# Who issues the first loads, and in which order VectorE, TensorE and GpSimd start, in an attention and expert kernel

## The chip, the cores and the metric

The kernel runs on one core of a Trainium2 chip. A core has five engines with an instruction queue each: TensorE (PE, matmuls and transposes), VectorE (DVE), ScalarE (ACT), GpSimd (POOL) and SyncE (SP), which in this kernel does nothing but issue DMAs. An engine works through its queue strictly in order: an instruction that waits for a semaphore holds up all that stands behind it. The DMAs themselves run on 16 DMA engines. The metric is the time of one execution in microseconds (us); lower is better.

## The reference

`x` is (8, 512, 256), float32. The reference does two residual blocks:

```
x = x + layernorm(attention(layernorm(x)))      # 16 heads of 16
x = x + layernorm(experts(layernorm(x)))        # 8 experts, top 1
```

The attention is not the usual one: the weights of each row are summed over the keys (`einsum('blmh,blhd->blhd')`), so that a head needs only the sum of its softmax row times its own `v`. The scores, their row maximum, the exponential and its sum must still be computed for 8 batches, 16 heads and 512 x 512 scores. The expert block is one shared matrix `wi` (256 to 1024) with a rank-4 correction of the chosen expert, a relu, and `wo` (1024 to 256).

## The kernel before

All matmuls are float32. Where precision asks for it a tensor is split into a high part (type fp32r) and a low part, and three products are summed: high by high, high by low, low by high (`three`, around L486). That is why names come in pairs: `wqkh`/`wqkl`, `xnh`/`xnl`, `wih`/`wil`.

**The stages of one batch b.** `prepare` normalises `x[b]`: the statistics `st_x_b` (4 pieces, L399) and `mv_x_b` (L404) on VectorE, the reciprocal root `nr_x_b` on GpSimd, the scaled `ln_x_b` (on VectorE for batch 0, on GpSimd for the others), a transpose on TensorE (`pst_xn`, L469), and the split into `xnh` (ScalarE, L521) and `xnl` (VectorE, L528). `project` multiplies by `wqk`, four products of 512 columns, each 6 matmuls: `psqk_b_g_t`, with g for the heads 0 to 7 or 8 to 15 and t = 0 for q, 1 for k. Each is split into `hl_b_g_t`; for batch 0 the high half is ScalarE's (L362) and the low half VectorE's (L375). `lay_out_q` and `lay_out_k` are DMAs from SBUF to SBUF: they put the rows of two heads, a pair p of 8, where the score matmul wants them. `rows_b_p` (L572, two DMAs) are the keys. The queries are `q_0_p` (L593, two DMAs) for the first 256 tokens of batch 0, and elsewhere a ring of six tiles q0 to q5 (L606, four DMAs each). `scores` then runs for each pair p and each 128 tokens: the score matmuls (`sc`, L651 for `q_0_p`, L642 for the ring), the negated row maximum `nmax` on VectorE (L661), and the exponential with its row sum on ScalarE (L670). A name such as `nmax_0_3_1_1` is batch 0, pair 3, token block 1, second head of the pair. `values`, `attend` and `feed` are the rest: `psv` and `v`, the division and the output projection `psy`, the gate (`wga`), and the expert matmuls `psh` and `psz`. A weight is split once at the start: `wvh`, `wvl`, `wouth`, `woutl`, `wih`, `wil`, `woh`, `wol` on GpSimd (L298, L306), `wqkl` and the LoRA factors `lbh`, `lbs` on VectorE (L306, L1166, L1171).

**What sets the order.** A planner (`Plan.order`) lists all operations by a model of costs and due times. `settle` then rewrites the start of that list by hand. Its helper `behind(last, ops)` takes `ops` out of the list and puts them directly after `last`. Each engine runs its own operations in the order of the list; the position of an operation therefore only counts against others of the same engine, and `behind` an operation of another engine means: at that place of the list. In the changed version `k0` and `q0`, `q1`, `k1` are the low halves of `hl_0_0_1`, `hl_0_0_0`, `hl_0_1_0` and `hl_0_1_1`. In the list of before, SyncE issues x of batch 0 in two halves, `wqk` in two, `bqk`, then `wv_0`, `wout_0`, `lb`, four `wi`, `xt_1` to `xt_3`, six small ones, then `q_0_0`, `rows_0_0`, `q_0_1`, `rows_0_1`, the four `wo`, `q_0_2`, `rows_0_2`, `rows_0_3` and so on.

**Two things that the list doesn't show.** Each DMA reports its landing on one of eight counters, which the framework hands out in turn, in the order of the list; a DMA whose counter is still owed by the DMA eight places earlier waits at its queue for that landing. And the PSUM tiles named `w` (for `pst`, `psqk`, `psv` and others) are three, used in turn: a fourth product waits until the first has been read. The scores have five.

The constants that the change touches or uses: `XB = 4` tiles of x, `X1B = 3` tiles for `q_0_p`, `QB = 6`.

Of the kernel before, what the change touches and what calls it, by code (L numbers as in the profile page):

```python
# [26 lines left out]
PE, ACT, DVE, POOL, DMA = "PE", "ACT", "DVE", "POOL", "DMA"  # L27
# [155 lines left out]
def kernel(  # L183
# [18 lines left out]
    nc = tc.nc  # L202
# [45 lines left out]
    def const_tile(shape, dtype, name, parts=1):  # L248
        return plan.tile(const, shape, dtype, name, 1, name)
# [6 lines left out]
    behind = [0.0]  # L256

    def landing(size):

        behind[0] = max(0.0, behind[0] + size / DMA_RATE - DMA_COST)  # L260
        return DMA_DELAY + size / DMA_RATE + behind[0]

    def load_x(b):
        t = xts[b] = plan.tile(io, [P, NC, D], F32, "xt", XB, f"xt_{b}")
        m = X0 if b == 0 else NC
        for c in range(0, NC, m):
            plan.op(
                DMA, DMA_COST,
                lambda c=c: nc.sync.dma_start(
                    out=t()[:, c : c + m],  # L270
                    in_=x[b].rearrange("(p c) d -> p c d", c=NC)[:, c : c + m],
                ),
                writes=[t], lag=landing(m * P * D * 4),
            )

    def load(name, src, shape=None, rows=P, place=None):

        shape = shape or list(src.shape)
        if place is None:
            t = const_tile(shape, F32, name)  # L280
        else:
            t = plan.tile(place[0], shape, F32, *place[1:], name)
        plan.op(
            DMA, DMA_COST, lambda: nc.sync.dma_start(out=t()[:rows], in_=src), writes=[t],
            lag=landing(rows * np.prod(src.shape[1:]) * 4),
        )
        return t

    def on_all_partitions(name, src):
        return load(name, src.partition_broadcast(P), [P, src.shape[0]])  # L290
# [23 lines left out]
    def fetch(name, src, *places):  # L314

        fs = flat(src).rearrange("p (c d) -> p c d", d=D)
        return [
            load(f"{name}_{i}", fs[:, 2 * i : 2 * i + 2], [P, 2, D], place=places[i % len(places)])
            for i in range(fs.shape[1] // 2)
        ]  # L320
# [23 lines left out]
    for i in range(2):  # L344
        t = const_tile([P, 2 * P], F32R, f"axs{i}")
# [146 lines left out]
    def units(b):  # L492

        return (0, 1), (2, 3)
# [590 lines left out]
    def fetch_first():  # L1085
        parts = [
            load(f"wqk_{dc}", wqk[:, dc], [P, 2, NG, P], place=(work, "full", FB))
            for dc in range(ND)
        ]
        return load("bqk", bqk), parts  # L1090

    during(-9000, "first", load_x, 0)
    wqk_in = during(-8990, "first", fetch_first)
    during(5000, "warm", warm_up)
# [36 lines left out]
    for g in range(NG):  # L1131
        during(-7000 if g == 0 else 0, f"project0{g}", project, 0, g)
        for p in range(NP * g, NP * (g + 1)):
            during(-6000 + 2 * p, "k0", lay_out_k, 0, p)
    during(0, "x1", load_x, 1)
    wv_h, wv_l = during(0, "wv", weight, "wv", wv.shape, wv_in, (POOL, POOL))

# [46 lines left out]
    for b in range(B):  # L1184
        t = 2 * STEPS * b
        if b + 2 < B:
            behind[0] = 0.0
            during(t, "load", load_x, b + 2)

        apart = units(b) if b in APART else [(0, 1, 2, 3)]  # L1190
        for i, cs in enumerate(apart):
            for p in range(NPR):
                at = t + STEPS * i + p * len(cs)
                during(at if b or i else at - 6000, "q" if b or i else "q0", lay_out_q, b, p, cs)
                scores(b, cs, p, at)
        if b + 1 < B:
            during(t, "prepare", prepare, b + 1)
            for g in range(NG):
                during(t, f"project{g}", project, b + 1, g)
                for p in range(NP * g, NP * (g + 1)):  # L1200
                    n = 2 if b + 1 in APART else 4
                    during(t + n * p, "k", lay_out_k, b + 1, p)
        for u in range(len(units(b))):
            tu = t + STEPS * (u if b in APART else 1)
            left = 2 * B - 1 - (2 * b + u)
            k = f"_{left}" if left < 3 else f"_first{u}" if b == 0 else f"{u}"
            during(tu, "v" + (k if b == 0 else ""), values, b, u)
            during(tu, "attend" + k, attend, b, u)
            during(tu, "feed" + k, feed, b, u)

    def settle(done):


        def of(eng, *marks):
            return [o for mark in marks for o in done if o.eng == eng and o.mark == mark]

        def behind(last, ops):
            for o in ops:
                done.remove(o)
            i = done.index(last) + 1  # L1220
            done[i:i] = ops


        behind(of(DVE, "ln_x_0_2")[-1], of(DVE, "bqk"))
        lbh = of(DVE, "lbh_0", "lbh_512")
        behind(of(DVE, "xnl_0")[-1], lbh)
        st2, turns = of(DVE, "st_x_2"), of(DVE, "hl_0_0_0", "hl_0_0_1", "hl_0_1_0")
        st1, maxes = of(DVE, "st_x_1"), of(DVE, "nmax_0_0_1_1", "nmax_0_2_0_1")
        behind(turns[0], st1[:2])
        behind(turns[1], st1[2:] + of(DVE, "mv_x_1"))  # L1230
        behind(turns[2], st2[:2])
        behind(maxes[0], st2[2:] + of(DVE, "mv_x_2"))
        behind(of(DVE, "nmax_0_2_0_1")[0], of(DVE, "st_x_3", "mv_x_3"))
        lbs = of(DVE, "lbs")
        behind(of(DVE, "nmax_0_1_1_1")[0], lbs[:1])
        behind(of(DVE, "nmax_0_3_0_1")[0], lbs[1:])
        behind(of(DVE, "nmax_0_4_1_1")[0], of(DVE, "wga"))


        nr = [[o for o in done if o.eng == POOL and o.mark == f"nr_x_{i}"] for i in range(4)]  # L1240
        wih, wil = of(POOL, "wih"), of(POOL, "wil")
        woh, wol = of(POOL, "woh"), of(POOL, "wol")
        behind(of(DVE, "mv_x_1")[-1], nr[1] + [wih[2], wil[2], wih[3], wil[3]])
        behind(of(DVE, "mv_x_2")[-1], nr[2])
        behind(of(POOL, "ln_x_2_2")[-1], nr[3])
        behind(
            [o for o in of(POOL, "ln_x_3_0")][-1], [woh[0], wol[0], woh[1], wol[1]]
        )
        behind(of(POOL, "hl_1_0_0")[-1], [woh[2], wol[2], woh[3], wol[3]])
        calm = Op()  # L1250
        calm.eng, calm.mark = POOL, None
        calm.fn = lambda: nc.gpsimd.tensor_scalar(
            calm_sb(), state[0]["xn"]()[:, 1, :1], 1.0, 0.0, ALU.mult, ALU.add
        )
        last = of(DVE, "ln_x_0_2")[-1]
        early = [o for o in done[done.index(nr[0][-1]) + 1 : done.index(last)] if o.eng == POOL]
        behind(last, early)
        done.insert(done.index(last) + 1, calm)


        rows = []
        for p in range(NP):
            if p < X1B:
                rows += of(DMA, f"q_0_{p}")
            rows += of(DMA, f"rows_0_{p}")
            if p == 1:
                rows += of(DMA, "wo_0", "wo_1", "wo_2", "wo_3")
        behind(turns[1], rows)


        extra = of(PE, "psu")[FIRST:]
        return [o for o in done if o not in extra]

    done = settle(plan.order())

    name = f"{B - 1}_{units(B - 1)[-1][0]}"
# [3 lines left out]
    i = [k for k, o in enumerate(done) if o.mark == f"mv_z_{name}_1"][-1] + 1  # L1280
# [66 lines left out]
DMA_COST = 440.0  # L1347
# [20 lines left out]
XB = 4  # L1368
HLB = 6
RB = 8  # L1370
QB = 6
# [69 lines left out]
```

## Time and profile before

| | |
|---|---|
| median of three runs | 516.54 us (516.49 to 519.35) |
| the profiled execution | 513.44 us |
| its span, from the first to the last instruction | 511.6 us |
| mean granted TensorE clock | 0.963 |
| TensorE, VectorE, ScalarE, GpSimd busy | 483.8, 467.3, 436.4, 390.1 us |
| the first score matmul starts | 21.11 us |
| the first exponential starts | 22.37 us |
| DMA issues on SyncE, each | 0.33 to 0.60 us |

The profile's page gives busy time by engine, the span in 40 equal slices of 12.8 us (a digit is the busy share in tenths; `PEclk` the clock that TensorE was granted), and the chain of work that ended last. Other views of the same trace list the instructions in order of time, the waits by who waited for whom, and the busy time in stretches that one chooses. A busy TensorE is not TensorE at full speed: a matmul that takes twice as long at half the clock counts as twice as busy.

### The profile page before, as it was taken

How to read it: one execution, taken by the hardware profiler on the slowest of the kernel's cores; microseconds unless marked ns; L12 is line 12 of the kernel's file. 1: busy time of each engine (PE TensorE's matmuls, PEld its weight loads, DVE VectorE, ACT ScalarE, POOL GpSimd, SP SyncE). 2: the span in 40 equal slices, each digit the busy share in tenths (PEclk: the TensorE clock that was granted, in tenths of full speed). 3: DMA queues.
4: the chain of work that ended last, by engine and by line, in shares of the span. 5: the costliest groups of instructions: out<-in, count | busy, mean ns of one | idle time of the engine just before them, and what ended most of it. 6: DMA issues, size and time to landing. Idle time of an engine off the chain costs nothing.

```text
span 511.6 us, 11203 instructions
## 1 busy us (share of the span) xinstructions
PE 483.8 (95%) x3134; PEld 423.7 (83%) x3134; DVE 467.3 (91%) x1056; ACT 436.4 (85%) x1205; POOL 390.1 (76%) x615
## 2 busy tenths in 40 slices
PE   7769989999999999999999999999999999998995
PEld 6534837879888988989989988989899988998995
DVE  6788999999999999999999999999999999998633
ACT  3569999998999999998999899999999989995210
POOL 7867455565889987997979998696878767888652
PEclk9955879999999999999999999999999999999999
DMA  8772263334423443244423442244224432200001
GB/s 273 217 196 68 52 154 71 89 69 112 111 51 106 113 111 68 69 121 104 105 50 120 101 102 75 51 113 110 66 70 94 114 87 67 48 26 2 21 22 42
DMA packets 41182, 46.56 MB, mean 91 GB/s; under 512 B 11326, under 2 KB 28222, under 8 KB 41120
## 3 DMA queue, kind: packets, MB, share of 16 engines
q1 hardware_dynamic: 41120, 45.84, 35.2%
q8 instruction: 26, 0.43, 0.3%
q14 instruction: 36, 0.29, 0.2%
HBM read 8.05 MB, written 4.19 MB: 24 GB/s over the span
## 4 chain that ended last, share of the span: by engine, by line
PE 62%; DVE 24%; ACT 4%; DMA 3%; issue 2%; SPq 2%; POOL 1%; POOLq 0%; ACTq 0%; DVEq 0%
PE sc L642 16%; PE psz L486 14%; DVE nmax L661 13%; PE psh L486 12%; PE psqk L486 7%; PE psy L486 3%; ACT sc L670 3%; PE psv L486 3%; PE psh L960 2%; DVE st_x L399 2%; PE sc L651 1%; DMA q<-hl 1%; DMA rows<-hl 1%; DVE hTh L300 1%; PE pst_x L469 1%
## 5 line engine op out<-in xcount | busy, mean ns | idle before, releaser
L670 ACT ACTIVATE sc<-sc,nmax 128x512 f32<-128x512 f32 x512 | 342.6, 689 | 17.1 <-DVE nmax L661 10.6
L661 DVE TENSOR_REDUCE nmax<-sc 128x1 f32<-128x512 f32 x512 | 325.4, 678 | 9.2 <-PE sc L651 4.2
L642 PE MATMUL sc<-rows,q 128*128 128x512 f32 x480 | 182.6, 423 | 5.6 <-ACT sc L670 3.1
L670 ACT ACTIVATION_READ_ACCUMULATOR sc<-sc,nmax 128x1 f32 x512 | 120.6, 236 | 0.0
L642 PEld LDWEIGHTS sc<-rows,q 128*128 128x128 f32 x480 | 88.7, 192 | 25.7 <-ACT sc L670 18.7
L486 PE MATMUL psz<-woh,hTh 128*128 128x256 f32 x256 | 73.0, 285 | 0.8 <-DVE xnl L528 0.5
L486 PE MATMUL psh<-x2h,wih 128*128 128x256 f32 x256 | 73.0, 285 | 0.0
L486 PE MATMUL psz<-woh,hTl 128*128 128x256 f32 x256 | 72.2, 282 | 0.0
L486 PE MATMUL psz<-wol,hTh 128*128 128x256 f32 x256 | 72.1, 282 | 0.0
L486 PE MATMUL psh<-x2h,wil 128*128 128x256 f32 x256 | 72.0, 281 | 0.0
L486 PE MATMUL psh<-x2l,wih 128*128 128x256 f32 x256 | 72.0, 281 | 0.0
L306 POOL TENSOR_TENSOR hTl<-full_h,hTh 128x512 fp32r<-128x512 f32 x44 | 56.9, 1294 | 2.3 <-DVE hTh L300 1.1
L486 PEld LDWEIGHTS psz<-wol,hTh 128*128 128x128 f32 x256 | 48.2, 188 | 3.6
L486 PEld LDWEIGHTS psh<-x2l,wih 128*128 128x128 f32 x256 | 48.2, 188 | 3.2
L486 PEld LDWEIGHTS psz<-woh,hTh 128*128 128x128 f32 x256 | 48.2, 188 | 2.1 <-POOL hTl L306 0.7
L486 PEld LDWEIGHTS psh<-x2h,wih 128*128 128x128 f32 x256 | 48.3, 189 | 1.1 <-DVE y L777 0.2
L486 PEld LDWEIGHTS psz<-woh,hTl 128*128 128x128 f32 x256 | 48.2, 188 | 0.2 <-POOL hTl L306 0.2
L486 PEld LDWEIGHTS psh<-x2h,wil 128*128 128x128 f32 x256 | 48.2, 188 | 0.0
L306 POOL TENSOR_TENSOR hl<-full_qk,hl 128x512 fp32r<-128x512 f32 x28 | 36.3, 1295 | 1.2
L384 ACT ACTIVATE full_h<-psh 128x512 f32<-128x512 f32 x44 | 26.4, 605 | 8.6 <-PE psh L960 8.1
L298 POOL TENSOR_SCALAR hl<-full_qk 128x512 fp32r<-128x512 f32 x28 | 17.3, 619 | 18.2 <-ACT full_qk L384 17.5
L486 PE MATMUL psqk<-xnh,wqkh 128*128 128x512 f32 x64 | 27.6, 431 | 0.7 <-ACT xnh L521 0.7
(132 smaller groups left out, 1021.4 us busy)
## 6 DMA issues: line engine op xcount, KB each, us to landing
rows<-hl SPq DMA_DIRECT2D x128, 128.0 KB, 2.6
q<-hl SPq DMA_DIRECT2D x480, 32.0 KB, 2.0
out<-ln_z SPq DMA_DIRECT2D x15, 256.0 KB, 2.2
xt<-in_x SPq DMA_DIRECT2D x7, 512.0 KB, 3.8
wi<-in_wi SPq DMA_DIRECT2D x4, 256.0 KB, 6.4
q<-hl SPq DMA_DIRECT2D x16, 64.0 KB, 2.2
wo<-in_wo SPq DMA_DIRECT2D x4, 256.0 KB, 4.5
xt<-in_x SPq DMA_DIRECT2D x2, 256.0 KB, 2.7
```

What stands on the lines that cost most here:

```text
L298: nc.gpsimd.tensor_scalar(pick_hi(), pick(), 1.0, 0.0, ALU.mult, ALU.add)
L300: nc.vector.tensor_copy(pick_hi(), pick())
L306: e.tensor_tensor(pick_lo(), pick(), f32(pick_hi()), ALU.subtract)
L384: lambda: nc.scalar.activation(full(), flat(ps()), func, **kw()),
L399: DVE, 335, lambda c=c: nc.vector.bn_stats(st()[:, c, :], sel()[:, c, :]),
L469: nc.tensor.transpose(ps()[:, dc, c * P : (c + 1) * P], src()[:, c, dc * P : (dc + 1) * P], ident(),)
L486: nc.tensor.matmul(ps, w, xx, start=start and i == 0, stop=stop and i == len(terms) - 1)
L642: nc.tensor.matmul(sc(), q()[:, e, cols], k(), start=True, stop=True)
L651: nc.tensor.matmul(sc(), q()[rows, 0, cols], k()[rows], start=True, stop=True)
L661: lambda sc=sc, nmax=nmax: nc.vector.tensor_reduce(nmax(), sc(), AX.X, ALU.max, negate=True),
L670: lambda sc=sc, nmax=nmax, esum=esum, i=i, h=h: nc.scalar.activation(sc(), sc(), AF.Exp, bias=nmax(), accum_out=esum()[:, i, h : h + 1]),
L960: nc.tensor.matmul(ps()[:, i, :], lbs()[:KL, fs], axs()[:KL, : n * P], start=False, stop=i == 1,)
```

## The change

Ten loads (`wv_0`, `wout_0`, `lb`, the four `wi`, `xt_1`, `xt_2`, `xt_3`) are issued by ScalarE's queue; the other loads stay on SyncE's. All 21 of them come directly behind `bqk`, and the four `wo` no longer stand between `rows_0_1` and `q_0_2`. The layout DMAs of pairs 0 to 3 stand behind `hl_0_0_1` rather than behind the first `hl` that is ready. VectorE gets another order of its first work, TensorE takes `psv` ahead of the last two `psqk`, ScalarE likewise `v` ahead of the last two `hl`, GpSimd takes `ln_x_1` ahead of the last `wi` splits. Later layout DMAs are exchanged: `q_0_6` and `q_0_7` come earlier, and the first 24 DMAs of the ring go tile by tile. Nothing is computed differently.

```diff
@@ load_x
-                lambda c=c: nc.sync.dma_start(
+                lambda c=c: (nc.scalar if 0 < b < XB else nc.sync).dma_start(
@@ load
+        queue = nc.scalar if name.split("_")[0] in ("wv", "wout", "lb", "wi") else nc.sync
...
-            DMA, DMA_COST, lambda: nc.sync.dma_start(out=t()[:rows], in_=src), writes=[t],
+            DMA, DMA_COST, lambda: queue.dma_start(out=t()[:rows], in_=src), writes=[t],
@@ settle
-        behind(of(DVE, "ln_x_0_2")[-1], of(DVE, "bqk"))
-        lbh = of(DVE, "lbh_0", "lbh_512")
-        behind(of(DVE, "xnl_0")[-1], lbh)
-        st2, turns = of(DVE, "st_x_2"), of(DVE, "hl_0_0_0", "hl_0_0_1", "hl_0_1_0")
-        st1, maxes = of(DVE, "st_x_1"), of(DVE, "nmax_0_0_1_1", "nmax_0_2_0_1")
-        behind(turns[0], st1[:2])
-        behind(turns[1], st1[2:] + of(DVE, "mv_x_1"))
-        behind(turns[2], st2[:2])
-        behind(maxes[0], st2[2:] + of(DVE, "mv_x_2"))
-        behind(of(DVE, "nmax_0_2_0_1")[0], of(DVE, "st_x_3", "mv_x_3"))
+        norms, wqkl, xnl = of(DVE, "ln_x_0_2")[-1], of(DVE, "wqkl"), of(DVE, "xnl_0")
+        behind(norms, of(DVE, "bqk") + wqkl[:1])
+        behind(xnl[0], wqkl[1:])
+        q0, k0, q1, k1 = of(DVE, "hl_0_0_0", "hl_0_0_1", "hl_0_1_0", "hl_0_1_1")
+        st = [of(DVE, f"st_x_{i}") for i in range(4)]
+        mv = [of(DVE, f"mv_x_{i}") for i in range(4)]
+        behind(q0, st[1][:2])
+        behind(k0, st[1][2:] + mv[1] + of(DVE, "lbh_0", "lbh_512") + st[2] + mv[2])
+        behind(of(DVE, "nmax_0_0_0_1")[0], [k1])
+        behind(of(DVE, "nmax_0_3_1_1")[0], st[3][:2])
+        behind(of(DVE, "nmax_0_4_0_1")[0], st[3][2:] + mv[3])
...
-        behind(of(DVE, "nmax_0_4_1_1")[0], of(DVE, "wga"))
+        behind(of(DVE, "nmax_0_2_3_1")[0], of(DVE, "wga"))
+        v = [[o for o in done if o.eng == eng and (o.mark or "").startswith(name)]
+             for eng, name in ((PE, "psv_0"), (ACT, "v_0"))]
+        behind(v[0][-1], of(PE, "psqk_0_1_0"))
+        behind(v[1][-1], of(PE, "psqk_0_1_1") + of(ACT, "hl_0_1_0", "hl_0_1_1"))
+        behind(of(ACT, "hl_0_1_0")[-1], [q1])
...
-        behind(of(DVE, "mv_x_1")[-1], nr[1] + [wih[2], wil[2], wih[3], wil[3]])
-        behind(of(DVE, "mv_x_2")[-1], nr[2])
-        behind(of(POOL, "ln_x_2_2")[-1], nr[3])
+        behind(of(DVE, "mv_x_1")[-1], nr[1])
+        behind(of(POOL, "ln_x_1_2")[-1], [wih[2], wil[2], wih[3], wil[3]])
+        behind(mv[2][-1], nr[2])
+        behind(mv[3][-1], nr[3] + of(POOL, "ln_x_3_0"))
...
-            if p == 1:
-                rows += of(DMA, "wo_0", "wo_1", "wo_2", "wo_3")
-        behind(turns[1], rows)
+        behind(
+            of(DMA, "bqk")[-1],
+            of(
+                DMA, "wv_0", "wout_0", "lb", "xt_1", "wi_0", "wi_1", "wi_2", "wi_3", "xt_2", "xt_3",
+                "bv", "low", "wo_0", "wo_1", "wo_2", "wo_3", "wga_f", "gb", "bout", "wob",
+            ),
+        )
+        behind(k0, rows)
+        behind(k1, of(DMA, "rows_0_4")[:1])
+        q5, q6, q7 = (of(DMA, f"q_0_{p}") for p in (5, 6, 7))
+        behind(q5[-1], of(DMA, "rows_0_7"))
+        behind(of(PE, "sc_0_3_1_0")[-1], q6)
+        behind(of(PE, "sc_0_4_1_0")[-1], q7)
+        names = [f"q{i}" for i in range(QB)]
+        at = [i for i, o in enumerate(done) if o.eng == DMA and o.mark in names][: 4 * QB]
+        pairs = sorted((done[i] for i in at), key=lambda o: o.n)
+        for i, o in zip(at, pairs):
+            done[i] = o
```

## The prediction

> **What bounds the kernel now.** I read the page's slices first: where is an engine idle, and where is TensorE slow?
>
> ```profile
> PE   7769989999999999999999999999999999998995
> DVE  6788999999999999999999999999999999998633
> ACT  3569999998999999998999899999999989995210
> PEclk9955879999999999999999999999999999999999
> DMA  8772263334423443244423442244224432200001
> ```
>
> From about 60 us to 460 us three engines are nearly full, and the list order there is untouched by the change. Slack lies in the first five slices: ScalarE at 3 to 6 tenths, and TensorE at half clock. So the change is worth what it shifts at the hand-over to that full stretch. The chain of work that ended last, in order of time, says what sets the start (start, duration, what):
>
> ```profile
> 1.64 4.38 DMA wqk<-in_wqk
> ...
> 11.02 2.97 DVE lbh L1166 x2
> ...
> 25.60 3.82 DMA rows<-hl
> ...
> 29.55 0.81 PE sc L651 x2
> 30.36 1.28 DVE nmax L661 x2
> 31.64 1.32 DVE st_x L399 x4
> ```
>
> The reader sees three things that the change attacks: the `lbh` casts in front of the first `hl`, the keys of pair 2 that land at 29.42, and the statistics of batch 3 inside pair 2's maxima. But the chain begins with `wqk`'s transfer, which the change does not shorten. Last, SyncE's waits (waited for: us in total, times, longest) and ScalarE's instructions in order of time:
>
> ```profile
> SPq L284 <- DMA lb<-in_lb: 1.5, 1, 1.5
> SPq L284 <- DMA wqk<-in_wqk: 1.0, 2, 0.7
> ...
> 0.72 1.28 ACT L1106 ACT_TABLE_LOAD   x1 [0.72 <-PEq L1425]
> 6.04 0.42 ACT L1106 ACTIVATE wqk<-wqk 128x256 f32<-128x256 f32 x1 [4.04 <-DMA wqk<-in_wqk]
> ```
>
> An issue waits for a landing: `lb` is the 8th DMA, and the 16th (`wga_f`, 10.71) waited for it. These are the eight counters. ScalarE is idle until 6.04, but not until later.
>
> **Step 1: ScalarE's queue, a loss.** Ten issues now stand ahead of ScalarE's first ACTIVATE. If the eight counters are handed out over both queues, the ten are the 6th to 15th DMA: `xt_1`, `wi_0` wait for the x halves, `wi_1`, `wi_2` for `wqk`, `wi_3` for `bqk`, `xt_2`, `xt_3` for `wv`, `wout`. In before `bqk` landed at 2.58 + 4.3 = 6.9. With that landing `wi_3`, `xt_2`, `xt_3` (0.43 + 0.57 + 0.57 and gaps, durations of SyncE's rows) end at 8.5. Lower bound for the issues alone: without any wait ten of 0.43 to 0.57 from 0.73 end at 5.6, which is hidden. Upper bound: the DMA engines are already busy (share 0.93 to 1.05 in every 2 us from 2 to 16 us, at 292 to 295 GB/s until 6 us), and now `wv`, `wout`, `lb` (0.92 MB) go beside x and `wqk` (1.05 MB). If they share equally, `wqk` and `bqk` land 0.92/0.292 = 3.2 us later, and ScalarE is free at 11.7.
>
> Then the table load of 1.28: it shares the line of the first ACTIVATE, so it may stand behind the ten (cost 1.28) or before (0); I take it behind, as the row has it next to that ACTIVATE. ScalarE's start then lies between 6.0 (loss 0) and 13.0 (loss 7); I take 11, a loss of 5, since both a wait and some sharing must occur, nearer the waits' 8.5 + 1.3 than the end of the sharing.
>
> The Trainium skill, "DMA: Bandwidth & Descriptors", section "Issuing engines are not separate DMA queues", says that DMAs of several issuers run on the same 16 engines and interleave, and that only issue time is saved. The trace agrees that the engines are full; by this rule the loss sits at the upper bound, 7 rather than 5, and my sum would end 2 us higher. "ScalarE: Activation LUTs" says that the compiler places the table load right before the ACTIVATE; by that the 1.28 is certain.
>
> **Step 2: from there to the keys of pair 0.** ScalarE had 1.04 of slack before `xnh` (idle until 9.13), so `xnh` is 4.0 late. VectorE's new order puts `wqkl[1]` (0.69) between the two `xnl`, after `xnh`: 13.76 + 0.67 + 0.69 + 0.67 = 15.8 where before had 11.10; the second `psqk` matmul is 4.7 late. TensorE now stands from the transposes to 15 with little work. In before the clock fell to half at 23, some 3.2 us after TensorE's block ended at 19.8, so I expect half clock: matmuls of 512 then follow each other in 0.43 rather than 0.23; over 8 to 12 of them 1.6 to 2.4, I take 1.8. (Kept clock: 0.) `k0`, the low half of `hl_0_0_1`, follows ScalarE's half directly, no longer behind `lbh`: 14.69 + 4.7 + 1.8 + 0.75 = 21.9, against 15.96. `psv` before the last `psqk` costs nothing by itself: the 24 `psv` (2.8) lie where TensorE would wait for rows.
>
> **Step 3: SyncE.** By the counters `gb` waits for `xt_3`; then `gb`, `bout`, `wob` (1.15) precede the first `q`. `xt_3` landed at 17.1 in before (the second `q_0_0` waited for it), and 1.05 MB of `wo` now shares the engines, at 400 GB/s (12 to 14 us) up to 2.6 us: `q_0_0` between 18.3 and 20.9, before 15.79. `rows_0_0` then goes at 21.9 (step 2), before 17.85. From there `rows_0_0`, `q_0_1`, `rows_0_1`, `q_0_2`, `rows_0_2` are ten issues of 0.63 without the four `wo` (2.0) between: the last starts at 27.6, and lands in 2.8 (median of the rows) instead of 3.82: 30.4 against 29.42, **1.0 late**. Between the ends of step 1: 4 early (k0 16.9) to 3 late.
>
> **Step 4: VectorE.** Between `k0` and the first maximum now stand two `st_x_1` (0.73), `mv_x_1` (0.35), two `lbh` (1.52 each as measured; at the least 0.67 each, the nearest VectorE row of 512 columns, `xnl`; I take the measured), `st_x_2`, `mv_x_2` (1.83), `q1` (0.75): 6.7. The first maximum comes at 28.6, before 21.65. Queued behind them wait all exponentials. Then pair 0 (2.48), `k1` (0.75), pair 1 (2.45), `lbs` (0.88): pair 2 at 35.2 against 30.36, 4.8 late (3.1 with casts of 0.67). Given back: the statistics of batch 3 (1.32 + 0.28) leave pair 2; they return behind pairs 3 and 4, where VectorE is idle for 1.5 between 42 and 50 us. So 4.8 - 1.6 = 3.2 late at pair 3, 1.6 more from the return, 1.5 absorbed: **3.3**.
>
> **Step 5: the rest.** `wga` and the exchanged ring DMAs: 0; the ring is first read at 50.2, and SyncE issues without large gaps from 16 to 66 in either order (bounds -0.6 to +0.6, one issue). GpSimd's `ln_x_1` before `wih[2..3]` could start up to 3.9 sooner, but its transposes stand behind pair 2's scores: 0. `wi` is first used by `psh` tens of us later. TensorE's half clock until 53.8 stays: the score matmuls of `q_0_p` are the same.
>
> **Sum.** TensorE 1.0, VectorE 3.3 late at the hand-over. VectorE is behind, and from 60 us it is full: I take **+3.0**. The profiled execution, span 511.6 and 1.84 around it, would be 516.4; its 513.44 lies 3.1 below the median shown, so against the median the forecast is **519.5**. The ends of step 1, carried through steps 3 and 4, give -1 and +6.
>
> **Rivals.**
>
> *A, faster, 0.28: the queue of ScalarE hides its issues.* If the counters don't hold ScalarE or `wqk` still lands at 6.0, ScalarE starts by 7.3, 1.04 of slack covers most, and `k0` is at 16.2. Then `rows_0_2` lands at about 26, 3.4 early, ScalarE's idle stretch of 2.68 before 31.14 goes, and the statistics free another 1.6; the first maximum is still held to 22.9 by step 4. Net -2 to -6, value -3.5: 513.0. For it speaks ScalarE's empty queue until 6.04; against it the full DMA engines and the visible waits eight places back. It decides from a ScalarE start below about 7.5.
>
> *B, clearly slower, 0.28.* Equal sharing of the DMA engines, table load behind, half clock over all twelve `psqk`: ScalarE 7 late, `k0` at 24.5, +6.5: 523.0. Nothing later has idle time to give back; TensorE is full at half clock until 53.
>
> *C, no change, 0.06.* VectorE's later start is eaten by TensorE's half-clock stretch (30 to 53 us, idle below 1 us), so that only TensorE's 1.0 counts, and that is lost in the rest: within 1 us, 516.5.
>
> **How the numbers follow.** The forecast has 0.38. A difference of 1% (5.2 us) is about what a measurement of this kernel can tell from no change. Forecast: all within 1% but 0.08 above. A: 0.14 beyond -1%, 0.14 within. B: 0.27 beyond, 0.01 within. C within. Faster 0.14, within 0.51, slower 0.35. The range runs from 512.5 (A's value and a little below) to 523.5 (B's value); outside are A's best cases and B's worst.
>
> **What would show it.** Right: the first ACTIVATE near 11 with DMA issues ahead of it, the second `psqk` matmul near 16, clock 0.5 around 15, first maximum near 28, no `wo` issue after 20, pair 2's maxima without a gap. Wrong in step 1: first ACTIVATE below 7.5. Wrong in step 3: `q_0_0` before 17. Wrong in step 5: the clock at 1.0 between 30 and 50 us, which would make TensorE short there and the kernel faster whatever the start.

## The result, and the profile after

| | before | after |
|---|---|---|
| median of four runs | 517.2 us (516.49 to 519.35) | 524.35 us (522.29 to 527.17) |
| ratio, 95% interval | | 1.0136 [1.0100, 1.0172] |
| profiled execution, its span | 513.44, 511.6 us | 522.29, 520.5 us |
| first ACTIVATE of ScalarE | 6.04 us | 14.90 us |
| second `psqk` matmul | 11.16 us | 19.64 us |
| first `q_0_0` issue, end of `k0` | 15.79, 15.96 us | 23.67, 25.59 us |
| first row maximum (`nmax`) | 21.65 us | 30.16 us |
| first `nmax` of pair 3 | 34.92 us | 40.17 us |
| first score matmul of the ring | 50.15 us | 56.41 us |

The changed kernel is slower by 7.1 us, 1.4%. The forecast had the sign, but only 3.0 us (counted from 516.54, the median of the first three runs), and the result lies just above its range of 512.5 to 523.5. The nearest value is rival B's (523.0 us), but the largest part of ScalarE's delay is not B's equal sharing of the DMA engines: it is waits, as E3 and E9 below show. The loss begins in the first two of the page's 40 slices, where ScalarE (ACT) stands at 0 and 4 tenths and VectorE (DVE) at 3 and 4:

```profile
PE   5589988999999999999999999999999989999995
DVE  3499899999999999999999999999999989998643
ACT  0478999999899999998999899999999988996110
PEclk9675697999999999999999999999999999999999
DMA  8564245234423443244422543244223442200001
```

The chain of work that ended last, again as start, duration, what, begins no longer with `wqk`. Two loads of ScalarE's own queue follow each other, then its last issue and the table load (the ACT piece of L1107 at 13.61):

```profile
1.65 6.84 DMA lb<-in_lb
8.49 0.02 issue
8.51 4.71 DMA wi<-in_wi
13.22 0.02 issue
13.24 0.33 ACTq L269
13.58 0.03 issue
13.61 1.28 ACT L1107
...
24.08 2.84 PE psv L487 x24
26.92 2.77 PE psqk L487 x12
29.70 0.47 PE sc L652 x2
```

`wi` at 8.51 is `wi_1`, the 13th DMA: it waits for the 5th, `lb`. L269 at 13.24 is `xt_3`, the 21st, which waits for `wi_1`. So the eight counters do go over both queues. With a single queue they are dealt in the order of the list, as said of the kernel before; with two, the framework merges the queues in an order of its own, and in the changed program ScalarE's ten are number 1, 3, 5, 8, 12, 13, 14, 16, 18 and 21. ScalarE's waits (waited for: us in total, times, longest) name the landing that came last. The 13.6 us are all the time since the start of the span; against the kernel before the price is 8.9 us (14.90 less 6.04):

```profile
ACT L1107 <- DMA wi<-in_wi: 13.6, 1, 13.6
```

### The profile page after: what moved, and what is told of

It reads as the page before. It is cut to its first block, busy times and chain, and to the rows that moved or that the text cites. A ratio compares the mean times of both kernels' runs of the same rounds, so it can differ in the third digit from the quotient of the medians.

```text
span 520.5 us, 11205 instructions
## 1 busy us (share of the span) xinstructions
PE 488.3 (94%) x3134; PEld 425.9 (82%) x3134; DVE 467.5 (90%) x1056; ACT 437.3 (84%) x1205; POOL 388.6 (75%) x615
## 4 chain that ended last, share of the span: by engine, by line
PE 64%; DVE 25%; DMA 4%; ACT 3%; issue 2%; POOL 1%; SPq 0%; ACTq 0%; POOLq 0%; DVEq 0%
PE sc L643 16%; DVE nmax L662 15%; PE psz L487 14%; PE psh L487 12%; PE psqk L487 8%; PE psy L487 3%; PE psv L487 3%; ACT sc L671 2%; PE psh L961 2%; DMA lb<-in_lb 1%; PE sc L652 1%; DVE st_x L400 1%; PE psg L812 1%; PE psg L815 1%; DMA wi<-in_wi 1%
## 5 line engine op out<-in xcount | busy, mean ns | idle before, releaser
L671 ACT ACTIVATION_READ_ACCUMULATOR sc<-sc,nmax 128x1 f32 x512 | 119.0, 233 | 0.0
```

The source lines that it names most:

```text
L671: lambda sc=sc, nmax=nmax, esum=esum, i=i, h=h: nc.scalar.activation(sc(), sc(), AF.Exp, bias=nmax(), accum_out=esum()[:, i, h : h + 1]),
```

## The experiments

Every kernel was timed beside the kernel before, and each ratio is to the runs of that kernel taken with it. Their medians were 518.63 us for E1 to E4, 515.82 for E5 to E8, and 517.24 for E9 and E10.

**E1, all loads back on SyncE, everything else of the change kept.** The theory after the result: ScalarE's waits make the whole loss. The rivals: the new compute orders make a part of it, or they hide a gain.

```diff
-        (nc.scalar if 0 < b < XB else nc.sync).dma_start(
+        nc.sync.dma_start(
...
-        queue = nc.scalar if name.split("_")[0] in ("wv", "wout", "lb", "wi") else nc.sync
+        queue = nc.sync
```

> The changed kernel with all its loads on SyncE's queue again; list positions and all orders as changed. Queue theory (ScalarE's issues wait for landings eight counters back, and its first ACTIVATE stands behind them): ScalarE's first ACTIVATE is back at about 6 us, the second psqk matmul at about 11, the whole 7 us shorter than the changed kernel and within 1.5 us of the kernel before. Order theory (the new orders, or the wo loads ahead of the first q, cost the time): ScalarE starts at 6 all the same, but the whole stays 3 us or more above the kernel before.

Measured: 518.22 us, ratio 0.9994 [0.9959, 1.0029]. The first ACTIVATE is at 5.67, the first maximum at 25.35, pair 3 at 34.82 and the ring at 51.08. The loss is gone, and so is any gain: ScalarE starts as early as before, and the new orders bring nothing.

**E2, the complement: the kernel before with the two queue lines alone.**

```diff
-                lambda c=c: nc.sync.dma_start(
+                lambda c=c: (nc.scalar if 0 < b < XB else nc.sync).dma_start(
...
+        queue = nc.scalar if name.split("_")[0] in ("wv", "wout", "lb", "wi") else nc.sync
...
-            DMA, DMA_COST, lambda: nc.sync.dma_start(out=t()[:rows], in_=src), writes=[t],
+            DMA, DMA_COST, lambda: queue.dma_start(out=t()[:rows], in_=src), writes=[t],
```

> The kernel before with nothing but the two lines that give ten loads to ScalarE's queue; list and orders as before. Here seven loads stand ahead of ScalarE's first ACTIVATE, the three xt behind it. Queue theory: the last of the seven waits for the landing of the first wi, about 9 us, then the table load of 1.28: ScalarE starts at 10.5 to 11.5, and the whole is 3 to 5 us above the kernel before. Order theory: ScalarE may start late, but the whole is within 1.5 us of the kernel before.

Measured: 525.51 us, ratio 1.0143 [1.0071, 1.0215]. The first ACTIVATE is at 11.20, the ring at 55.54. The two lines alone make the loss, and more of it than the 3 to 5 us expected. ScalarE starts 3.7 us sooner than after the change, yet the ring is read only 0.9 sooner: when ScalarE is late, the new orders do give something back. They do not when it is early (E1).

**E3, only `wv`, `wout`, `lb` and `xt_1` on ScalarE.** Those four need no earlier landing, but the bytes that go beside `wqk` are there. This separates the waits from the sharing of the DMA engines.

```diff
-        (nc.scalar if 0 < b < XB else nc.sync).dma_start(
+        (nc.scalar if b == 1 else nc.sync).dma_start(
...
-        queue = nc.scalar if name.split("_")[0] in ("wv", "wout", "lb", "wi") else nc.sync
+        queue = nc.scalar if name.split("_")[0] in ("wv", "wout", "lb") else nc.sync
```

> The changed kernel with only wv, wout, lb and xt_1 on ScalarE's queue, which hold the first eight counters together with SyncE's first four and wait for nothing; the four wi, xt_2 and xt_3 are SyncE's. It keeps the sharing of the DMA engines and takes the waits off ScalarE. Waits theory: ScalarE's first ACTIVATE comes with wqk's landing, about 8.3 us instead of 14.9, and 4 to 5 us of the changed kernel's 7 go. Sharing theory (the two queues' sharing alone makes the loss): wqk's two halves land at 8.3 and 10.3 as in the changed kernel, and at most 2 us of the 7 go.

Measured: 519.22 us, ratio 1.0029 [0.9993, 1.0064]. ScalarE's instructions in order of time (start, duration, line, operation; in brackets the idle time before it and what ended it):

```profile
2.74 1.28 ACT L1107 ACT_TABLE_LOAD   x1 [2.74 <-issue]
8.36 0.42 ACT L1107 ACTIVATE wqk<-wqk 128x256 f32<-128x256 f32 x1 [4.34 <-DMA wqk<-in_wqk]
```

The reader sees the table load directly behind the four issues, and an ACTIVATE that waits for `wqk` itself. The sharing is real: the halves of `wqk` land 6.7 and 8.2 us after their issue (4.4 and about 4.6 before), and ScalarE is 2.3 us late. But hardly any of it reaches the end. The other 6.5 us of ScalarE's delay, from 8.36 to 14.90, are waits and the table load behind them.

**E9, `lb` as the last of ScalarE's ten issues.** Same bytes, same engines, same number of issues, other waits. By the program's counters `lb` is now number 25 and waits for `xt_2`, which waits for `bqk`.

```diff
-                DMA, "wv_0", "wout_0", "lb", "xt_1", "wi_0", "wi_1", "wi_2", "wi_3", "xt_2", "xt_3",
+                DMA, "wv_0", "wout_0", "xt_1", "wi_0", "wi_1", "wi_2", "wi_3", "xt_2", "xt_3", "lb",
```

> The changed kernel with one move: lb is the last of ScalarE's ten issues instead of the third. No more and no fewer bytes, issues or engines. By the program's counters xt_2 now waits for bqk, and lb, as the 25th DMA, waits for xt_2's landing. Theory of the waits: wi_1 and wi_2 no longer wait for lb, but the last issue waits for two landings in a row again: bqk near 9 to 10 us, xt_2 issued near 10.8, landing 4.4 to 7.7 us later at 15.2 to 18.5, then the table load of 1.28; the first ACTIVATE comes at 17 to 20 us instead of 14.90, and the kernel is 2 to 5 us slower than the changed one (ratio to before 1.017 to 1.023). Theory of the sharing: the bytes are the same and lb now goes out of wqk's way, so wqk lands earlier and the first ACTIVATE comes at or before 14.9; ratio 1.014 or less. Theory that the orders alone make the loss: 1.014 with the first ACTIVATE anywhere.

Measured: 527.08 us, ratio 1.0185 [1.0121, 1.0248], the first ACTIVATE at 17.72, the ring at 58.98. The chain of this kernel (start, duration, what):

```profile
0.72 3.92 DMA wv<-in_wv
4.64 0.02 issue
4.66 4.96 DMA bqk<-in_bqk
9.62 0.02 issue
9.64 6.15 DMA xt<-in_x
15.80 0.02 issue
15.82 0.58 ACTq L285
16.40 0.03 issue
16.43 1.28 ACT L1107
```

Three landings in a row now (`wv`, `bqk`, `xt_2`) before `lb` can go, as the counters say, and ScalarE starts 2.8 us later than after the change, inside the expected 17 to 20. The sharing theory, by which it would start no later than 14.9, falls. For the whole, the ratio (1.0185) lies in the expected 1.017 to 1.023, but its interval overlaps that of the change (1.0100 to 1.0172), so the 2.8 us are shown at ScalarE's start and at the ring (2.6 later), not at the end.

**E4, the table load ahead of the waits.** A copy of one column behind `xt_1`'s issue, into a tile that nothing reads, brings the table load forward.

```diff
+        early = Op()
+        early.eng, early.mark = ACT, None
+        early.fn = lambda: nc.scalar.activation(table_sb(), mhalf()[:, :1], AF.Copy)
+        done.insert(done.index(of(DMA, "xt_1")[-1]) + 1, early)
```

> The changed kernel with one tiny activation on ScalarE directly behind its fourth load, so that the activation table is loaded while ScalarE waits for counters. If ScalarE's start is on the path that sets the end: first wqk ACTIVATE at 13.6 instead of 14.9, and the whole 0.8 to 1.3 us shorter than the changed kernel. If its lateness is absorbed later: no difference.

Measured: 523.77 us, ratio 1.0117 [1.0058, 1.0177]. The load is at 2.76, the first ACTIVATE at 13.06, the ring at 54.49, 1.9 us sooner than after the change in both places. Of the 1.84 us at ScalarE, 1.28 are the load itself; the last issue also ends 0.6 us sooner (13.01 against 13.58). The whole is too close to the changed kernel's to tell apart.

**E5, E7, E8: the new orders and the place of the `wo` loads, without ScalarE's queue.** E5 is E1 with the loads and the `wo` also placed as in the kernel before, so that only the new orders of the compute engines and of the layout DMAs are left. E7 is E5 with the four `wo` behind `rows_0_3`. E8 is the kernel before with that alone.

```diff
-        behind(
-            of(DMA, "bqk")[-1],
-            of(
-                DMA, "wv_0", "wout_0", "lb", "xt_1", ...
-            ),
-        )
...
+            if p == 1:
+                rows += of(DMA, "wo_0", "wo_1", "wo_2", "wo_3")
```

In E7 the condition is `p == 3`, and E8, from the kernel before, is only this:

```diff
-            if p == 1:
+            if p == 3:
                 rows += of(DMA, "wo_0", "wo_1", "wo_2", "wo_3")
```

> The changed kernel with its loads as before: all on SyncE, in the positions of before, wo between rows_0_1 and q_0_2; only the new orders of VectorE, TensorE, ScalarE, GpSimd and of the ring's DMAs remain. Theory that the new orders gain what the prediction's steps 4 and 5 say: first q at about 15.8, first maximum at 22 to 23, the statistics of batch 3 gone from pair 2, the whole 1 to 2.5 us below the kernel before. Theory that the orders cost or are absorbed: within 1 us of the kernel before, or above.

> As e5_orders, but the four wo loads stand behind rows_0_3. If the wo loads in front of pair 2's keys are what holds pair 2 in the kernel before: rows_0_2 lands at 26 to 27 instead of 29.4, pair 2's first maximum at about 29, the whole 2 to 4 us below the kernel before. If TensorE at half clock or VectorE bounds pairs 2 to 7 whatever the keys: no more than e5_orders, within 1 us of it.

> The kernel before with the four wo loads behind rows_0_3 and nothing else changed. If the wo loads hold pair 2: rows_0_2 lands at 26 to 27 and the whole is 1.5 to 3 us below the kernel before. If the statistics of batch 3 and the casts on VectorE then bound pair 2: within 1 us of the kernel before.

Measured: E5 516.77 us, ratio 1.0023 [0.9996, 1.0051]; E7 518.12 us, 1.0027 [0.9985, 1.0069]; E8 516.05 us, 1.0016 [0.9995, 1.0038]. None is faster. E8 shows where the keys' gain goes (VectorE's instructions in order of time, and one row of TensorE's):

```profile
28.11 1.27 DVE L661 TENSOR_REDUCE nmax<-sc 128x1 f32<-128x512 f32 x2
...
34.43 1.29 DVE L661 TENSOR_REDUCE nmax<-sc 128x1 f32<-128x512 f32 x2 [1.69 <-PE sc L651]
...
33.63 0.79 PE L651 MATMUL sc<-rows,q 64*128 64x512 f32 x2 [4.00 <-DMA rows<-hl]
```

Pair 2's maxima are 2.2 us earlier than before (28.11 against 30.35). Pair 3's are 0.5 earlier, after an idle 1.69 us in which VectorE waits for the scores. TensorE itself stood idle for 4.00 us before these scores, until a layout DMA landed (the profile names one of `rows`, issued at 29.85, behind the `wo`); in E7 it is 3.95 us and the same releaser. With the `wo` behind `rows_0_3` the wait has moved from pair 2 to pair 3, and TensorE's half clock is not what holds it there. The ring's first score comes at 50.46 (50.15 before), at 50.76 in E5 and at 50.40 in E7. In every kernel whose ScalarE starts by 8.4 us it lies between 50.1 and 51.4.

**E6, E10: more warm-up matmuls, to price TensorE's half clock.** After the change TensorE is granted 0.50 of its clock from 14 to 22 us. 30 warm-up matmuls stand at its start; E6 has 70 of them, as below, and E10 has 96. In both only 68 run ahead of `psqk`, by the kernel's own order, so E10 gave no larger warm-up there than E6.

```diff
-FIRST = 30
+FIRST = 70
```

> The changed kernel with 70 warm-up matmuls instead of 30, so that TensorE is busy until about 15 us and does not fall to half clock before its first psqk. If the half clock was part of the loss: granted clock 1.0 from 0 to 24 us, the first two psqk products 1.7 us shorter, and the whole 1 to 2 us below the changed kernel, that is about 5.5 us above the kernel before. If that stretch is absorbed: no difference from the changed kernel's 7 us.

> The changed kernel with 96 warm-up matmuls instead of 30; with 70 they ended at 13.0 us and the clock fell at about 16.7, just before psqk. At 0.13 us each the 26 more end at about 16.4, so TensorE has work until the first psqk matmul near 17.5. If the half clock costs what step 2 took (1.8 us): psqk matmuls 0.23 apart instead of 0.43, k0 and the first maximum 1.6 to 2.4 us earlier than in the changed kernel (near 28.3 instead of 30.16). Theory that the start is passed on: the whole is 1.5 to 2 us shorter than the changed kernel, ratio 1.010. Theory that pairs 2 to 7 absorb it: the first ring score stays near 56 and the ratio near 1.014. If the warm-ups themselves get in the way of psqk, the first psqk matmul is later than 17.97.

Measured: E6 524.8 us, ratio 1.0175 [1.0147, 1.0203]; E10 525.75 us, 1.0186 [1.0123, 1.0249]. Neither put `psqk` under the full clock. In E6 the matmuls end at 13.0 and the clock is 0.64 at 16 to 18 us and 0.50 behind it. In E10 they end at 12.6, and the other 28 run between 28.9 and 34.6 us among the first scores, and the first maximum slips from 30.16 to 33.62. TensorE's work, clock and the rest by stretches of E10 (stretch, its length, busy time of PE, PEld, DVE, ACT and POOL with instructions, granted clock, DMA share, GB/s):

```profile
12.00:14.00 2.00, 0.61 (x6) 0.40 (x4) 0.30 (x1) 0.55 (x1) 2.00 (x3) 1.00 0.92 234
14.00:16.00 2.00, 0.00 (x0) 0.00 (x0) 0.15 (x1) 1.96 (x4) 1.92 (x3) 0.76 0.98 307
16.00:18.00 2.00, 0.19 (x1) 0.19 (x1) 1.24 (x3) 1.73 (x4) 1.59 (x2) 0.50 1.02 410
```

So the whole's price of the half clock stays open; only its price on TensorE can be read (below). What E10 adds is another delay at the start, 2.9 us at the ring (59.32); at the end its ratio can't be told from the change's (1.0136).

The runs side by side, by ScalarE's start:

| kernel | first ACTIVATE | first `nmax` | ring's first score | ratio to before |
|---|---|---|---|---|
| E8 (old orders) | 5.65 | 21.59 | 50.46 | 1.0016 |
| E1 | 5.67 | 25.35 | 51.08 | 0.9994 |
| E5 | 5.75 | 22.03 | 50.76 | 1.0023 |
| E7 | 5.79 | 21.50 | 50.40 | 1.0027 |
| before | 6.04 | 21.65 | 50.15 | 1 |
| E3 | 8.36 | 25.34 | 51.40 | 1.0029 |
| E2 (old orders) | 11.20 | 28.34 | 55.54 | 1.0143 |
| E4 | 13.06 | 28.25 | 54.49 | 1.0117 |
| E6 | 14.15 | 30.13 | 56.16 | 1.0175 |
| E10 | 14.74 | 33.62 | 59.32 | 1.0186 |
| after | 14.90 | 30.16 | 56.41 | 1.0136 |
| E9 | 17.72 | 32.78 | 58.98 | 1.0185 |

E5 and E1 have the same compute orders: a first maximum 3.3 us later (25.35 against 22.03) is caught up by the ring but for 0.3. What is later than about 25.4 goes on to the ring one for one: in E1, E3, E4, E6, after, E9 and E10 the ring comes 25.7 to 26.3 us behind the first maximum. At the end these late kernels lose about as much as at the ring, or somewhat more (after: 6.3 at the ring, 7.1 at the end; E9: 8.8 and 9.8).

## Why the prediction was wrong, step by step

**Step 1 is the one that failed, in its size.** The mechanism was right: ten issues stand ahead of ScalarE's first ACTIVATE and wait for landings. The term that was mis-sized is the wait. I had ScalarE's issues wait only for the early loads (the x halves, `wqk`, `bqk`, `wv`, `wout`) and end at 8.5, between which and an upper end of 13.0 I took 11. In the program one of them, `wi_1`, waits for another of ScalarE's own, `lb`, and the last, `xt_3`, for `wi_1` in turn: 6.84 + 4.71 in series, up to 13.58, then the table load. ScalarE starts at 14.90, 8.9 us late and not 5, 1.9 beyond my upper end. By parts: sharing 2.3 (E3; my bound was 3.2), table load 1.84 of ScalarE's start (E4; 1.28 its own time), and the remaining 4.7, a difference that no run measured by itself, the chain of waits. The table load does stand behind the ten issues, as I took it. (In the rows of before the DMA engines' share goes up to 1.06, not 1.05, which changes nothing.) The upper end was no upper end, because it counted the eight places in the order of the list, where the ten are number 6 to 15 and wait for x, `wqk`, `bqk`, `wv` and `wout`, and took the landings from before; in the order that the program has, ScalarE's own late loads hold the counters.

The Trainium skill, "DMA: Bandwidth & Descriptors", section "Issuing engines are not separate DMA queues", says that DMAs of several issuers share the 16 engines. By it the forecast would have ended 2 us higher and nearer to the result, but not for the right reason: E3 agrees with the sharing and measures only 2.3 us of the 8.9 for it.

**Step 2 held.** From its +5 at ScalarE I had the second `psqk` matmul 4.7 late; with 8.9 it is 8.5 late. `k0`, expected 5.95 late, is 9.63 late, which is 5.95 + 3.9 less 0.2. The half clock came as expected, at 0.50 from 14 to 22 us, with the `psqk` matmuls 0.43 apart where they were 0.23.

**Step 3 held where it could be seen.** In the changed kernel `q_0_0` waits for VectorE, not for SyncE, and is issued at 23.67. E1 shows SyncE's own bound: 19.79, inside 18.3 to 20.9. Behind `k0` the `wo` and the rest give back 3.9 us until `rows_0_2` is issued (30.72 against 24.96), where I had 3.95.

**Step 4 was nearly right in its net, and three of its terms were off.** From `k0` to the ring 3.3 us are given back (9.63 late, then 6.3); I had 2.65 (5.95, then 3.3). VectorE's instructions of the changed kernel:

```profile
26.44 0.73 DVE L1167 CAST lbh<-lb 98x512 fp32r<-98x512 f32 x2
...
30.16 1.29 DVE L662 TENSOR_REDUCE nmax<-sc 128x1 f32<-128x512 f32 x2 [0.34 <-PE sc L652]
32.02 3.67 DVE L662 TENSOR_REDUCE nmax<-sc 128x1 f32<-128x512 f32 x6
...
36.82 2.47 DVE L662 TENSOR_REDUCE nmax<-sc 128x1 f32<-128x512 f32 x4
```

The casts `lbh` take 0.73 for both, not 3.04; from `k0` to the first maximum it is 4.6 us, not 6.7. And it isn't VectorE that ends this wait: the chain above has `psv`, twelve `psqk` and the first scores in a row on TensorE up to 30.17. Given back between the first maximum and pair 3 are 3.3 us (8.5 late, then 5.25), where I had 3.75. From there to the ring 1.0 is lost again (6.3 late), where I had 0.1. That 1.0 belongs to the new orders and not to the queue: from pair 3's first maximum to the ring it takes 16.2 to 16.3 us in all nine kernels that have them, late or not, and 15.2 in before and in E2 (E8, with the old orders and a sooner pair 3, has 16.0). Which of the new orders costs it was not taken apart.

**Step 5 held as far as it was seen.** The half clock in the scores of `q_0_p` stays (0.50 from 44 to 52 us in both), and E5, the orders and the ring's exchange without the rest, stands at +0.23% [-0.04%, 0.51%].

**The sum.** B's +6.5 is 0.6 more than its terms add up to (3.3, and 2.6 for a `k0` at 24.5 instead of 21.9, make 5.9); the +6 at the upper end of step 1 is likewise more than 3.3 and the 2 us of later start make. With ScalarE 1.9 later than B's 7 and 2.3 us less for the casts, 6.5 gives 6.1 at the hand-over, and 5.9 gives 5.5. Measured are 6.3 at the ring and 7.1 between the medians. That it closes so well is partly luck: the casts did not end the wait for the first maximum, the new orders cost 1.0 behind pair 3, and the two profiled executions differ by 8.9.

**The rivals.** A (513.0) fails twice. ScalarE does start late; and where it doesn't, nothing is won (E1, E5, E7, E8). Its price of 3.5 us counted the earlier keys of pair 2 and the freed statistics as a gain of the whole, and pair 3 takes them back by waiting for its scores. In E7 and E8 those scores wait with TensorE idle for a layout DMA, as the row above shows; in the other kernels it was not taken apart. C's thought, that this stretch swallows what is won or lost ahead of it, is right for a first maximum up to about 25.4 us (E5 against E1); the loss was larger than that. That TensorE's half clock is what swallows it, as C has it, is not shown.

## What to carry to other kernels

A DMA that a compute engine issues may cost that engine far more than its issue: when completion counters are shared, an issue waits for the landing of an earlier DMA, and everything behind it in that engine's queue waits too. Before loads are moved to a compute engine, write down for each which DMA holds its counter in the new order, and follow the chain; only as many loads as need no such wait (four here) are nearly free, and nothing was won even by those. And a gain at the start is worth something only if the next stretch isn't bound by another engine: follow it to the first wait that doesn't move, here pair 3's for its scores.

## What was not expected of the hardware

The cast `lbh` (98x512, float32 to fp32r) takes 1.52 us in the kernel before and 0.41 in the changed one, with the same operands. Groups by tile (operation, count: duration in ns, least, median and most, first and last start), before and after:

```profile
L1166 DVE CAST lbh<-lb x2: 1518/1525/1532, 11.0 to 12.5; 98x512 fp32r<-98x512 f32 x2
```

```profile
L1167 DVE CAST lbh<-lb x2: 396/410/425, 26.4 to 26.8; 98x512 fp32r<-98x512 f32 x2
```

What GpSimd did beside the two slow ones, in the kernel before:

```profile
10.99 1.28 POOL L306 TENSOR_TENSOR wvl<-wv,wvh 128x512 fp32r<-128x512 f32 x1
12.23 1.48 POOL L306 TENSOR_TENSOR woutl<-wout,wouth 128x512 fp32r<-128x512 f32 x1
```

The first cast ends at 12.5, 0.3 us after `wvl` ends; the second at 13.99, 0.3 after `woutl`. After the change GpSimd stands idle from 17.2 to 26.6 us, and beside the casts it has only instructions on 128x4 elements. In E1 one cast took 0.47, the other 1.50 beside a GpSimd subtraction. So these 2.3 us look like a wait for GpSimd inside VectorE's recorded busy time, and a duration from one schedule didn't hold in another. The changed kernel has the same on its chain: the first `wqkl` takes 1.77 us where it took 0.69 before, and ends 0.5 us after a GpSimd subtraction that started beside it:

```profile
15.97 1.27 POOL L307 TENSOR_TENSOR wil<-wi,wih 128x512 fp32r<-128x512 f32 x1
16.01 1.77 DVE L307 TENSOR_TENSOR wqkl<-wqk,wqkh 128x512 fp32r<-128x512 f32 x1 [5.07 <-ACT wqkh L303]
```

The Trainium skill, "SBUF — State Buffer", section "SBUF: two separate sides", says that VectorE in some modes and GpSimd hold a shared pair of ports exclusively, the loser waiting for the whole instruction. That is what these rows look like; no run here varied it by itself.

The other is the clock: in E6 TensorE's matmuls followed each other from 1.7 to 13.0 us at the full clock, and yet the idle time behind them was enough for it to fall to half. From the 0.64 of the slice 16 to 18, and 1.00 and 0.50 on either side of it, the fall came near 16.5 (an estimate). In E10 the matmuls end at 12.6 and the slice 14 to 16 has 0.76, so the fall came near 15. The idle time ahead of it was thus 3.5 us in one run and 2.4 in the other: the 3.2 that step 2 read in the kernel before, where four score matmuls ran in between, is no fixed delay.
